# The order of the step lists of a two-layer graph kernel, head, loop and tail written anew

## The chip, the core and the metric

The kernel runs on one core of one Trainium2 chip. It is one launch that handles all 32 batches. The metric is device time in microseconds; the time before is the median of three runs.

The core's engines run side by side, each through its own list of instructions in order: TensorE (PE, matmuls), VectorE (DVE), ScalarE (ACT), GpSimd (POOL) and the queue of SyncE (SP), which issues most transfers. An engine that waits for another's result holds up everything behind in its own list, and nothing else.

## The reference

The inputs are x (32 batches of 512 x 1024) and one matrix adj (512 x 512) that serves as weight in both layers; all in float32. Cut to what matters:

```
# layer 0: attention over the 1024 columns, with rank-one scores
q = einsum('c,bcn->bn', wq, x);  k = einsum('c,bcn->bn', wk, x)
scores = leaky_relu(q[:, None, :] + k[:, :, None], 0.01)
agg = einsum('bcn,bmn->bcm', x, softmax(scores, -1))
x = layernorm(x + relu(einsum('oc,bcm->bom', adj, agg) + bm[:, None]))
# layer 1
x = layernorm(x + einsum('bnf,nm->bmf', x, adj * adj) + bias)
```

## The kernel before, in words

The attention matrix is never formed. As a score is q plus k, and the slope changes where the sum changes sign, the softmax of a column is a sum over all columns with a larger q, with one weight, and over the rest with another. So the kernel sorts the columns by q, builds running sums of the weighted columns from both ends, and looks up for each k the two running sums at its place. Per batch b, with the names of the steps as the lists have them (the dictionary `ops` gives the function of each, and a word such as `z.0.2` is step `z`, batch 0, part 2):

- `ld` (L87) loads x in four transfers. x has four buffers, so four batches are in flight. `pa` (L247) forms q and k on PE, `pc` copies them out, `co` turns them, `cc` (L267) copies the columns. `qw` (L275) writes q as a row to DRAM, and `ro` (L283) reads it back for all 128 partitions into qb, which has one buffer.
- `rk` (L308, DVE, eight parts) finds each column's rank by q, `re` makes them whole numbers; `ct` (L323, ACT, eight parts) counts for each k the columns on its other side, `ce` ends it.
- `z` (L346, PE) is the product of x and adj for 128 columns, and `zc` (L352, ACT) copies it into the table zt, of which there is one. In batches 1 to 30 only parts 0 to 3 are formed so; the other half is formed by a scheme of seven quarter products (`zU`, `zV`, `zY`, `z11`, `zZ`, `z12`, `z21`, L390) with sums `x1` to `x4` on DVE before, and copies or additions (`zUc`, `zVc`, `zZc`, `zup`, `zlr`, `zll`) between and after.
- `sc` (L451, POOL, eight parts) scatters the rows of zt to their ranks in DRAM. `tb` (L289) reads the largest q back, `tp` forms the differences to it, `we` their weights. `sl` (L470) loads the sorted rows, in two halves, into the one tile tab. `se` gives their weights.
- `u` (L491) and `d` (L501), eight each, are the running sums up and down within a partition; the first of each is ACT's. `cu` and `cd` (L509, PE) carry them over the partitions; `uc`, `te`, `dc` copy the carries; `tu` and `td` (L538, DVE) add them. `tw` (L553) and `tl` (L556) write the table to DRAM.
- `g` (L563, POOL, eight parts) gathers two rows for each column. `mw` forms the mixing weights; `ms` (L585, ACT) and `mx` (L590, DVE) mix. `t` (L609, PE) turns the result, `r` (L617, DVE) adds x, `s0` (L600, ACT), `rt`, `rce` and `n0` (L635, ACT) are the first layernorm, in four parts.
- Layer 1 is again seven products per half (`U`, `V`, `Y`, `11`, `Z`, `12`, `21`, L665, L667 and L702), twice, with `t1` to `t4` (L646 to L660) before them and copies and sums (`Uc`, `Vc`, `Zc`, `up`, `lr`, `ll`, `ls`) behind. `s1`, `ra`, `rb`, `r1` and `n` are the second layernorm, the small ones on POOL, and `st` (L777) stores the batch in four parts.

Nothing is moved by a scheduler. The order of the words in three lists of text, `head`, `loop` and `tail`, is the order in which the steps are written out, and each engine's own order is the words of its steps in that order. Buffers follow from it too: PSUM has four slots for z, q and k, the carries and the layer 1 sums, and two double ones for the quarter pairs, the turned results and the layer 1 pairs, and a tile takes a slot whose last user stands earlier in the lists. `emit` (L802) writes a list out with a base added to the batch numbers: the head with 0, the loop for each b of a range, the tail with 32. In the kernel before, the head has 2439 words, the loop 194, written five times, and the tail 2787. Where two scatters follow each other on POOL, a tiny memset (L449) is put between.

Of the kernel before, what the change touches and what calls it, by code (L numbers as in the profile page):

```python
# [49 lines left out]
def adj_resnorm_kernel(  # L50
# [759 lines left out]
    ld.0 ldw.0 pa.0 pc.0 qw.0 ld.1 wt.0 ro.0 ld.3 wd.0 wc.0 co.0 z.0.2 cc.0 rk.0.0 ct.0.2 pa.1  # L810
    zc.0.2 x3.1 ct.0.3 rk.0.7 z.0.3 ct.0.1 rk.0.4 ct.0.6 rk.0.1 ct.0.7 oq.0 rk.0.5 z.0.5 ct.0.5
    rk.0.6 R.0 z.0.4 zc.0.5 ct.0.0 pc.1 rk.0.2 qw.1 ld.2 rk.0.3 co.1 z.0.0 re.0 cc.1 bias.0
    sc.0.5 z.0.7 zc.0.0 zc.0.3 ct.0.4 sc.0.3 ro.1 sc.0.0 z.0.1 zc.0.7 zc.0.4 sc.0.4 rk.1.1
    ct.1.3 sc.0.2 z.0.6 zc.0.1 x1.1 ct.1.6 rk.1.0 sc.0.7 x2.1 rk.1.6 z11.1 sc.0.1 zc.0.6 rk.1.5
    zU.1 sc.0.6 rk.1.7 pa.2 rk.1.2 x4.1 zZ.1 rk.1.3 pc.2 zUc.1 qw.2 ct.1.4 tb.0 sl.0.0 zV.1
    sl.0.1 ct.1.1 ct.1.0 z.1.2 x1.2 ce.0 rk.1.4 zVc.1 tp.0 se.0.0 zZc.1 z.1.3 u.0.0 u.0.1 u.0.2
    se.0.1 ct.1.7 u.0.3 x2.2 co.2 ct.1.5 zY.1 u.0.4 oq.1 u.0.5 zc.1.3 ct.1.2 cc.2 z12.1 u.0.6
# [466 lines left out]
```

## Time and profile before

| | |
|---|---|
| median of three runs | 1941.6 us (1938.44 to 1947.02) |
| the profiled execution | 1942.71 us |
| its span in the trace | 1940.9 us, 23403 instructions |
| mean granted TensorE clock | 0.993 |
| busy: PE, DVE, ACT, POOL | 1887.8, 1704.6, 1483.5, 897.2 us |
| HBM read and written | 287.08 and 269.42 MB, 287 GB/s over the span |

The profile is one execution. Its busy times are sums over the span, so they hide where an engine waits: the kernel has a start in which batches come in one after the other, a long middle in which four batches overlap, and an end in which they run out. Views of a stretch (busy time by window, the timeline of one engine, the chain of waits) answer for the stretch. A bracket at the end of a timeline row gives the idle time before it and what ended it.

### The profile page before, as it was taken

To read this page: it belongs to the slowest core of one execution; us is meant where nothing else is said; L and a number is where in the kernel's file an instruction comes from. 1 tells how busy PE (TensorE), PEld (TensorE's weight loads), DVE (VectorE), ACT (ScalarE), POOL (GpSimd) and SP (SyncE) were. 2 spreads that over 40 slices of the span, in tenths; PEclk is the share of its full clock that TensorE was granted. 3 is DMA by queue.
4 is the path that set the end of the run, shared out by engine and by line. 5 is a ranking of instruction groups with operands and counts; after the bars stand their busy time and mean duration, and the time that the engine had idled before them with its cause. 6 is when DMAs were issued, how large, how long until landed. Compare 5 with 4: busy or idle time off the path is not lost.

```text
span 1940.9 us, 23403 instructions
## 1 busy us (share of the span) xinstructions
PE 1887.8 (97%) x7073; PEld 1072.0 (55%) x7073; DVE 1704.6 (88%) x2746; ACT 1483.5 (76%) x2663; POOL 897.2 (46%) x1074
## 2 busy tenths in 40 slices
PE   7988999999999999999999999999999999999897
PEld 3654555555555555566555566555565555554443
DVE  6897899998899889989988989988998989889973
ACT  3566677878778777778787778787777787877786
POOL 5263435335434345454456454455443355445531
PEclk9999999999999999999999999999999999999899
DMA  6577788677888687877787887777888677887862
GB/s 250 197 290 271 286 309 339 253 294 282 313 310 315 252 309 270 331 307 291 290 306 280 317 311 304 277 299 286 308 312 310 262 291 300 308 320 279 331 245 95
DMA packets 147446, 558.05 MB, mean 288 GB/s; under 512 B 19653, under 2 KB 19793, under 8 KB 139129
## 3 DMA queue, kind: packets, MB, share of 16 engines
q1 hardware_dynamic: 89936, 354.40, 48.4%
q0 software_dynamic: 57344, 202.15, 27.6%
q8 instruction: 56, 0.92, 0.2%
q14 instruction: 70, 0.57, 0.1%
q10 hardware_dynamic: 40, 0.02, 0.0%
HBM read 287.08 MB, written 269.42 MB: 287 GB/s over the span
## 4 chain that ended last, share of the span: by engine, by line
PE 78%; DMA 8%; DVE 7%; issue 2%; ACT 2%; POOL 2%; SPq 0%; POOLq 0%; DVEq 0%; ACTq 0%
PE z_ps L346 19%; PE sum_ps L667 18%; PE pair_ps L667 10%; PE z_sum_ps L390 9%; PE z_pair_ps L390 7%; PE pair_ps L702 5%; PE agg_ps L609 4%; DMA table<-tab 3%; PE qk_ps L247 3%; DMA tab<-sorted_z 2%; DVE tab L538 2%; PE carry_ps_True L509 1%; PE carry_ps_False L509 1%; DMA x<-in_x_dram 1%; DMA sorted_z<-zt,to 1%
## 5 line engine op out<-in xcount | busy, mean ns | idle before, releaser
L563 POOL DMA_INDIRECT got<-table,of x256 | 302.3, 1181 | 568.8 <-DMA table<-tab 260.6
L346 PE MATMUL z_ps<-adj_t,x 128*128 128x512 f32 x1088 | 486.9, 594 | 1.4 <-DVE qkc L267 1.1
L451 POOL DMA_INDIRECT sorted_z<-zt,to x256 | 314.0, 1226 | 176.7 <-issue 73.9
L308 DVE SCALAR_TENSOR_TENSOR junk_v<-qb,qkc,tie 128x1024 uint8<-128x1024 f32 x256 | 329.8, 1288 | 10.0 <-DMA qb<-q_row 6.4
L346 PEld LDWEIGHTS z_ps<-adj_t,x 128*128 128x128 f32 x1088 | 202.3, 190 | 225.5 <-issue 212.4
L323 ACT ACTIVATE junk_s<-qb,qkc 128x1024 uint8<-128x1024 f32 x256 | 293.4, 1146 | 19.7 <-DMA qb<-q_row 14.3
L667 PE MATMUL sum_ps<-zt,S 128*128 128x512 f32 x512 | 236.1, 593 | 3.1 <-DVE zt L651 1.4
L585 ACT ACTIVATE got<-got,w 128x512 f32<-128x512 f32 x256 | 172.6, 718 | 42.2 <-DVE w L580 41.8
L590 DVE SCALAR_TENSOR_TENSOR got<-got,w 128x512 f32<-128x512 f32 x256 | 185.6, 746 | 12.0 <-ACT got L585 11.8
L491 DVE SCALAR_TENSOR_TENSOR tab<-tab,ac 128x514 f32<-128x514 f32 x192 | 144.6, 753 | 49.8 <-ACT tab L486 29.2
L617 DVE SCALAR_TENSOR_TENSOR x<-agg_ps,small,x 128x1024 f32<-128x1024 f32 x128 | 163.1, 1280 | 23.9 <-PE agg_ps L609 23.6
L600 ACT ACTIVATE junk<-g,tv 128x1024 uint8<-128x1024 f32 x128 | 146.9, 1148 | 32.9 <-DVE g L722 26.4
L501 DVE SCALAR_TENSOR_TENSOR tab<-tab,ac 128x513 f32<-128x513 f32 x224 | 167.5, 748 | 2.6 <-ACT tab L499 1.9
L667 PEld LDWEIGHTS sum_ps<-zt,S 128*128 128x128 f32 x512 | 96.5, 190 | 121.6 <-issue 105.8
L753 POOL TENSOR_SCALAR tv<-tv 128x1 f32<-128x1 f32 x124 | 53.1, 428 | 238.5 <-ACT junk L600 230.5
L774 ACT ACTIVATE g<-g,nb,tv 128x1024 f32<-128x1024 f32 x124 | 151.0, 1237 | 7.3 <-POOL nb L764 7.2
L600 ACT ACTIVATE junk<-x,tv 128x1024 uint8<-128x1024 f32 x128 | 146.9, 1148 | 12.2 <-DVE x L617 9.9
L538 DVE TENSOR_TENSOR tab<-tab,carry 128x2052 f32<-128x2052 f32 x64 | 146.2, 2291 | 4.7 <-ACT carry L516 4.7
L635 ACT ACTIVATE x<-x,tv 128x1024 f32<-128x1024 f32 x128 | 139.3, 1141 | 0.5
L609 PEld LDWEIGHTS agg_ps<-ident,got 128*128 128x128 f32 x1024 | 116.4, 141 | 36.2 <-issue 24.9
L609 PE MATMUL agg_ps<-ident,got 128*128 128x128 f32 x1024 | 129.4, 274 | 2.7 <-DVE g L722 2.0
L667 PE MATMUL sum_ps<-x,adj 128*128 128x512 f32 x256 | 123.3, 605 | 7.4 <-ACT x L635 7.4
(144 smaller groups left out, 3281.5 us busy)
## 6 DMA issues: line engine op xcount, KB each, us to landing
table<-tab SPq DMA_DIRECT2D x64, 2056.0 KB
tab<-sorted_z SPq DMA_DIRECT2D x64, 1028.0 KB
x<-in_x_dram SPq DMA_DIRECT2D x128, 512.0 KB
out_dram<-g SPq DMA_DIRECT2D x128, 512.0 KB
qb<-q_row SPq DMA_DIRECT2D x32, 512.0 KB
sorted_z<-zt,to POOLq DMA_INDIRECT x256, 5.0
got<-table,of POOLq DMA_INDIRECT x256, 8.0
adj_in<-in_adj_dram SPq DMA_DIRECT2D x1, 1024.0 KB
```

Source lines behind the costliest of these rows:

```text
L308: nc.vector.scalar_tensor_tensor(s.junk, s.qb, s.q[:, j : j + 1], tie[:, at : at + N], ALU.subtract, ALU.is_gt, accum_out=s.rank[:, j : j ...
L323: nc.scalar.activation(junk, s.qb, AF.Sign, bias=s.k[:, j : j + 1], accum_out=s.sign[:, j : j + 1])
L346: nc.tensor.matmul(s.z[j], xt[:, c, j * P : (j + 1) * P], adj_t[:, c, :], start=(c == 0), stop=(c == CT - 1),)
L390: nc.tensor.matmul(ps, a[:, i, k * P : (k + 1) * P], v[:, i, :], start=start and i == 0 and (k == 0 or bank == 1), stop=(i == 1), skip_gro ...
L451: nc.gpsimd.indirect_dma_start(out=sorted_z[b % 2][:, :], out_offset=bass.IndirectOffsetOnAxis(ap=s.to[:, j : j + 1], axis=0), in_=zt[:, j ...
L538: nc.vector.tensor_tensor(v, v, c, ALU.add)
L563: nc.gpsimd.indirect_dma_start(out=s.got[:, j, :], out_offset=None, in_=table[b % 2][:, :], in_offset=bass.IndirectOffsetOnAxis(ap=s.of[:, ...
L585: nc.scalar.activation(down, down, AF.Copy, scale=s.w[:, 1, j : j + 1])
L590: nc.vector.scalar_tensor_tensor(up, up, s.w[:, 0, j : j + 1], down, ALU.mult, ALU.add)
L600: nc.scalar.activation(junk, t, AF.Square, bias=v[0][:, i : i + 1], scale=-float(N), accum_out=v[1][:, i : i + 1],)
L609: nc.tensor.transpose(s.agg[o][:, j * P : (j + 1) * P], s.got[:, j, o * P : (o + 1) * P], ident)
L667: nc.tensor.matmul(ps, a[:, k, g * P : (g + 1) * P], v[:, k, :], start=False, stop=(k == 1), skip_group_check=first is None,)
```

## The change

The three lists are replaced by others. Both programs hold the same 6196 steps, each on its engine; the place of the steps in the order differs. The head now has 2633 words and the loop is written eight times, for batches 15 to 22 in place of 14 to 18; the tail has 2011. As fewer scatters stand next to each other, 161 of the small memsets are there in place of 164. Shown are the start of the head, its part around the first layer 1, the whole loop, and a part of the tail; the rest is of the same kind.

```diff
     head = """
-    ld.0 ldw.0 pa.0 pc.0 qw.0 ld.1 wt.0 ro.0 ld.3 wd.0 wc.0 co.0 z.0.2 cc.0 rk.0.0 ct.0.2 pa.1
-    zc.0.2 x3.1 ct.0.3 rk.0.7 z.0.3 ct.0.1 rk.0.4 ct.0.6 rk.0.1 ct.0.7 oq.0 rk.0.5 z.0.5 ct.0.5
-    rk.0.6 R.0 z.0.4 zc.0.5 ct.0.0 pc.1 rk.0.2 qw.1 ld.2 rk.0.3 co.1 z.0.0 re.0 cc.1 bias.0
-    sc.0.5 z.0.7 zc.0.0 zc.0.3 ct.0.4 sc.0.3 ro.1 sc.0.0 z.0.1 zc.0.7 zc.0.4 sc.0.4 rk.1.1
-    ct.1.3 sc.0.2 z.0.6 zc.0.1 x1.1 ct.1.6 rk.1.0 sc.0.7 x2.1 rk.1.6 z11.1 sc.0.1 zc.0.6 rk.1.5
-    zU.1 sc.0.6 rk.1.7 pa.2 rk.1.2 x4.1 zZ.1 rk.1.3 pc.2 zUc.1 qw.2 ct.1.4 tb.0 sl.0.0 zV.1
-    sl.0.1 ct.1.1 ct.1.0 z.1.2 x1.2 ce.0 rk.1.4 zVc.1 tp.0 se.0.0 zZc.1 z.1.3 u.0.0 u.0.1 u.0.2
-    se.0.1 ct.1.7 u.0.3 x2.2 co.2 ct.1.5 zY.1 u.0.4 oq.1 u.0.5 zc.1.3 ct.1.2 cc.2 z12.1 u.0.6
-    zlr.1 zc.1.2 ro.2 u.0.7 z.2.2 re.1 zup.1 d.0.7 d.0.6 sc.1.4 x3.2 d.0.5 sc.1.2 cu.0 d.0.4
-    z21.1 d.0.3 te.0 sc.1.3 uc.0 tl.0 ct.2.2 tu.0.0 z.1.0 we.0 zll.1 d.0.2 ct.2.4 sc.1.7 rk.2.1
...
-    tu.1.0 zc.3.3 cd.1 zVc.3 dc.1 zY.3 oq.3 ct.3.7 mx.0.7 sc.3.1 td.1.0 ct.3.5 z12.3 ms.0.6
-    td.1.1 z.3.0 ms.0.5 tw.1.0 ms.0.4 tu.1.1 zc.3.0 zlr.3 tw.1.1 mx.0.5 tb.2 z21.3 mx.0.6 mx.0.4
-    zup.3 zll.3 t.0.2 r.0.2 t.0.1 sc.3.4 r.0.1 sc.3.7 t.0.3 s0.0.2 r.0.3 sc.3.0 t.0.0 s0.0.1
-    r.0.0 sc.3.6 s0.0.3 sl.2.0 sl.2.1 tp.2 sc.3.5 s0.0.0 g.1.3 rt.0 rce.0 n0.0.0 g.1.2 n0.0.1
-    g.1.1 se.2.0 U.0.0 t1.0 g.1.0 u.2.0 n0.0.2 u.2.1 u.2.2 n0.0.3 g.1.5 u.2.3 U.0.1 t2.0 Uc.0.0
-    g.1.7 se.2.1 t4.0 11.0.0 Uc.0.1 g.1.4 u.2.4 t3.0 V.0.0 g.1.6 u.2.5 mw.1.0 Z.0.0 sc.3.2
-    Vc.0.0 u.2.6 ms.1.0 u.2.7 ms.1.1 sc.3.3 Y.0.0 ce.3 mx.1.0 Zc.0.0 d.2.7 mx.1.1 ms.1.3 d.2.6
-    11.0.1 d.2.5 mw.1.1 12.0.0 d.2.4 ms.1.5 tb.3 lr.0.0 ms.1.2 mx.1.3 V.0.1 mx.1.2 d.2.3 Z.0.1
-    Vc.0.1 up.0.0 ms.1.7 mx.1.5 21.0.0 tp.3 Zc.0.1 d.2.2 ms.1.6 ms.1.4 12.0.1 ll.0.0 mx.1.4
...
+    ld.0 ldw.0 ld.1 bias.0 pa.0 pc.0 qw.0 wt.0 wd.0 wc.0 co.0 z.0.2 ro.0 x1.1 cc.0 pa.1 rk.0.2
+    ct.0.0 rk.0.7 z.0.4 pc.1 ct.0.4 qw.1 rk.0.5 zc.0.2 ct.0.5 rk.0.0 ct.0.1 co.1 rk.0.1 z.0.0
+    ct.0.3 cc.1 rk.0.3 ct.0.6 rk.0.6 ct.0.7 z.0.5 rk.0.4 zc.0.4 ct.0.2 re.0 x2.1 oq.0 ro.1
+    sc.0.4 ld.2 z.0.3 zc.0.5 sc.0.5 sc.0.2 rk.1.3 ct.1.3 z.0.1 zc.0.3 R.0 ct.1.7 zc.0.0 sc.0.0
+    z.0.7 zc.0.1 ce.0 x3.1 sc.0.3 rk.1.0 sc.0.1 rk.1.6 z.0.6 zc.0.7 rk.1.2 ct.1.1 sc.0.7 rk.1.5
+    ct.1.6 x4.1 pa.2 zc.0.6 sc.0.6 z11.1 pc.2 ct.1.5 qw.2 zU.1 tb.0 sl.0.0 sl.0.1 co.2 zUc.1
+    zZ.1 tp.0 ct.1.4 rk.1.7 zV.1 zZc.1 rk.1.1 ct.1.2 z.1.2 x1.2 zVc.1 se.0.0 rk.1.4 u.0.0 ct.1.0
+    u.0.1 u.0.2 se.0.1 ro.2 z.1.3 zc.1.2 u.0.3 ld.3 x2.2 u.0.4 oq.1 cc.2 u.0.5 u.0.6 z12.1
+    zc.1.3 re.1 u.0.7 d.0.7 zY.1 zup.1 d.0.6 sc.1.4 cu.0 zlr.1 z.2.2 d.0.5 uc.0 sc.1.3 x3.2 te.0
+    d.0.4 tl.0 sc.1.5 d.0.3 x4.2 d.0.2 z21.1 rk.2.1 z.1.0 zll.1 d.0.1 ct.2.0 sc.1.7 d.0.0 ce.1
...
+    ct.3.4 r.0.2 t.0.1 sc.3.5 r.0.1 sc.3.0 t.0.3 s0.0.2 r.0.3 sc.3.7 t.0.0 s0.0.1 r.0.0 sc.3.4
+    s0.0.3 sl.2.0 sl.2.1 tp.2 sc.3.6 s0.0.0 g.1.3 rt.0 rce.0 n0.0.1 g.1.2 n0.0.0 g.1.1 se.2.0
+    U.0.1 g.1.0 u.2.0 n0.0.3 u.2.1 g.1.4 t1.0 n0.0.2 u.2.2 g.1.5 U.0.0 t2.0 u.2.3 g.1.7 11.0.0
+    Uc.0.0 t4.0 Uc.0.1 se.2.1 t3.0 g.1.6 V.0.0 u.2.4 ce.3 mw.1.0 11.0.1 sc.3.2 u.2.5 ms.1.1
+    ms.1.0 u.2.6 Z.0.0 ms.1.3 u.2.7 Vc.0.0 mx.1.3 d.2.7 mx.1.1 V.0.1 Zc.0.0 d.2.6 d.2.5 Y.0.0
+    mw.1.1 d.2.4 ms.1.6 12.0.0 ms.1.2 lr.0.0 ms.1.7 mx.1.0 ms.1.5 mx.1.2 Z.0.1 ms.1.4 up.0.0
+    d.2.3 21.0.0 Zc.0.1 mx.1.5 zc.3.3 d.2.2 mx.1.6 12.0.1 ll.0.0 mx.1.4 Vc.0.1 s1.0.0 ls.0.0
+    d.2.1 Y.0.1 ld.4 mx.1.7 s1.0.2 ra.0.0 cu.2 lr.0.1 ra.0.2 rb.0.0 up.0.1 t.1.2 uc.2 r1.0.0
+    sc.3.3 21.0.1 te.2 r.1.2 s1.0.1 d.2.0 t.1.1 n.0.0 ra.0.1 rb.0.2 t.1.3 r.1.1 ll.0.1 rb.0.1
+    cd.2 s0.1.2 r1.0.2 r1.0.1 tu.2.0 t.1.0 tb.3 s0.1.1 tl.2 z.4.3 st.0.0 r.1.3 dc.2 n.0.2 ls.0.1
+    tp.3 td.2.0 s1.0.3 st.0.2 zU.4 s0.1.3 ra.0.3 r.1.0 tw.2.0 rb.0.3 pa.4 r1.0.3 td.2.1 s0.1.0
+    we.3 z.4.2 tu.2.1 pc.4 n.0.3 qw.4 rt.1 st.0.3 rce.1 x1.4 n0.1.3 tw.2.1 z11.4 ro.4 zc.4.2
...
     """
     loop = """
-    z.0.0 s0.-3.0 x2.0 x3.0 rt.-3 tp.-1 rce.-3 ct.0.6 rk.0.7 ct.0.5 zV.0 oq.0 rk.0.2 g.-2.3
-    sl.-1.0 sl.-1.1 rk.0.3 zZ.0 zVc.0 g.-2.0 x4.0 zY.0 rk.0.6 zZc.0 g.-2.1 n0.-3.0 rk.0.0
-    n0.-3.1 z12.0 g.-2.2 zlr.0 n0.-3.2 t1.-3 U.-3.0 g.-2.5 n0.-3.3 re.0 zup.0 se.-1.0 ct.0.1
-    z21.0 sc.0.4 u.-1.0 sc.0.5 11.-3.1 Uc.-3.0 u.-1.1 ct.0.4 t2.-3 g.-2.7 zll.0 11.-3.0 u.-1.2
-    se.-1.1 u.-1.3 g.-2.6 V.-3.0 u.-1.4 mw.-2.0 g.-2.4 u.-1.5 ms.-2.2 U.-3.1 Vc.-3.0 u.-1.6
-    sc.0.6 ce.0 t3.-3 Z.-3.0 Uc.-3.1 sc.0.7 u.-1.7 ms.-2.3 ms.-2.0 sc.0.2 ms.-2.1 Z.-3.1 d.-1.7
-    mx.-2.1 sc.0.3 we.-1 mx.-2.2 Zc.-3.0 V.-3.1 d.-1.6 Zc.-3.1 mx.-2.3 d.-1.5 12.-3.1 Vc.-3.1
-    mw.-2.1 t4.-3 ms.-2.4 12.-3.0 ms.-2.6 up.-3.1 ms.-2.7 Y.-3.0 d.-1.4 ld.1 s1.-3.1 mx.-2.6
-    zc.0.1 ra.-3.1 Y.-3.1 zc.0.0 lr.-3.0 rb.-3.1 ms.-2.5 up.-3.0 r1.-3.1 sc.0.1 21.-3.0 lr.-3.1
-    s1.-3.0 sc.0.0 mx.-2.5 d.-1.3 21.-3.1 ll.-3.0 ra.-3.0 mx.-2.7 n.-3.1 rb.-3.0 d.-1.2 cu.-1
-    r1.-3.0 mx.-2.4 ll.-3.1 st.-3.1 d.-1.1 pa.1 uc.-1 ls.-3.1 ls.-3.0 d.-1.0 s1.-3.3 tu.-1.0
-    z.1.2 s1.-3.2 ra.-3.3 mx.-2.0 pc.1 rb.-3.3 te.-1 tu.-1.1 qw.1 tl.-1 r1.-3.3 t.-2.2 ro.1
-    zc.1.2 n.-3.0 cd.-1 ra.-3.2 r.-2.2 rb.-3.2 co.1 n.-3.3 t.-2.1 r1.-3.2 st.-3.0 cc.1 t.-2.3
-    dc.-1 r.-2.1 st.-3.3 n.-3.2 tb.0 z.1.3 td.-1.0 s0.-2.1 st.-3.2 ct.1.3 r.-2.3 tw.-1.0 ct.1.2
-    z.1.1 td.-1.1 zc.1.3 ct.1.7 rk.1.5 s0.-2.3 tw.-1.1 t.-2.0 x1.1 ct.1.0 zU.1 rk.1.4 r.-2.0
-    z11.1 zUc.1 s0.-2.2 rk.1.1
+    z.0.0 x3.0 zUc.0 x2.0 rt.-3 ct.0.5 oq.0 rk.0.7 rce.-3 rk.0.3 zV.0 g.-2.0 sl.-1.0 sl.-1.1
+    x4.0 zZ.0 rk.0.0 zVc.0 g.-2.3 ct.0.6 rk.0.2 zY.0 zZc.0 n0.-3.1 g.-2.1 tp.-1 rk.0.6 n0.-3.0
+    z12.0 g.-2.2 zlr.0 n0.-3.3 t1.-3 U.-3.0 g.-2.5 se.-1.0 n0.-3.2 re.0 zup.0 ct.0.1 z21.0
+    sc.0.4 u.-1.0 sc.0.5 11.-3.1 Uc.-3.0 u.-1.1 ct.0.4 t2.-3 g.-2.4 se.-1.1 11.-3.0 u.-1.2 zll.0
+    u.-1.3 g.-2.7 V.-3.0 u.-1.4 mw.-2.0 g.-2.6 u.-1.5 ms.-2.2 U.-3.1 Vc.-3.0 u.-1.6 sc.0.7 t3.-3
+    Z.-3.0 Uc.-3.1 u.-1.7 sc.0.6 ms.-2.0 mx.-2.2 ms.-2.3 ms.-2.1 Z.-3.1 sc.0.3 d.-1.7 mx.-2.1
+    Zc.-3.0 d.-1.6 sc.0.2 we.-1 V.-3.1 mx.-2.3 Zc.-3.1 d.-1.5 mw.-2.1 12.-3.1 t4.-3 ms.-2.7
+    Vc.-3.1 12.-3.0 ms.-2.4 up.-3.1 ms.-2.6 d.-1.4 s1.-3.1 Y.-3.0 ld.1 mx.-2.6 zc.0.1 ra.-3.1
+    zc.0.0 rb.-3.1 Y.-3.1 lr.-3.0 ms.-2.5 r1.-3.1 up.-3.0 sc.0.1 21.-3.0 lr.-3.1 sc.0.0 s1.-3.0
+    mx.-2.5 d.-1.3 21.-3.1 ra.-3.0 ll.-3.0 mx.-2.7 n.-3.1 rb.-3.0 d.-1.2 cu.-1 r1.-3.0 mx.-2.4
+    ll.-3.1 d.-1.1 pa.1 uc.-1 ls.-3.0 ls.-3.1 d.-1.0 s1.-3.3 tu.-1.0 z.1.2 te.-1 ra.-3.3 s1.-3.2
+    tl.-1 mx.-2.0 st.-3.1 rb.-3.3 tu.-1.1 pc.1 n.-3.0 qw.1 r1.-3.3 t.-2.2 st.-3.0 zc.1.2 ro.1
+    cd.-1 ra.-3.2 r.-2.2 n.-3.3 rb.-3.2 co.1 t.-2.1 r1.-3.2 dc.-1 cc.1 ce.0 st.-3.3 n.-3.2
+    t.-2.3 tb.0 r.-2.1 z.1.3 st.-3.2 td.-1.0 ct.1.0 s0.-2.1 r.-2.3 tw.-1.0 ct.1.2 z.1.1 rk.1.5
+    ct.1.7 td.-1.1 zc.1.3 ct.1.3 t.-2.0 s0.-2.3 rk.1.4 tw.-1.1 zU.1 s0.-2.2 x1.1 r.-2.0 z11.1
+    rk.1.1 s0.-2.0
     """
     tail = """
...
-    z.-1.6 r.-4.0 g.-3.6 rk.-1.2 g.-3.1 oq.-1 r.-4.1 se.-2.0 z.-1.4 u.-2.0 g.-3.5 we.-3 u.-2.1
-    s0.-4.1 u.-2.2 g.-3.3 zc.-1.5 ce.-1 u.-2.3 se.-2.1 re.-1 s0.-4.0 g.-3.2 z.-1.7 u.-2.4 u.-2.5
-    zc.-1.4 g.-3.0 rt.-4 u.-2.6 rce.-4 ce.-2 n0.-4.3 u.-2.7 g.-3.4 d.-2.7 zc.-1.7 d.-2.6 sc.-1.0
-    zc.-1.2 cu.-2 n0.-4.1 d.-2.5 d.-2.4 g.-3.7 n0.-4.0 d.-2.3 uc.-2 U.-4.1 mw.-3.0 sc.-1.7
-    zc.-1.6 d.-2.2 te.-2 tu.-2.1 n0.-4.2 tl.-2 sc.-1.2 st.-5.3 ms.-3.2 11.-4.1 n.-5.0 d.-2.1
-    mw.-3.1 n.-5.1 U.-4.0 st.-5.0 sc.-1.1 d.-2.0 ms.-3.6 t1.-4 st.-5.1 sc.-1.6 ms.-3.1 cd.-2
...
+    rt.-4 rce.-4 zc.-1.7 d.-2.7 g.-3.5 cu.-2 n0.-4.1 d.-2.6 g.-3.6 d.-2.5 zc.-1.4 n0.-4.0 d.-2.4
+    sc.-1.4 ce.-2 uc.-2 d.-2.3 U.-4.0 n.-5.0 mw.-3.0 sc.-1.2 d.-2.2 te.-2 U.-4.1 st.-5.0 tu.-2.1
+    n0.-4.2 sc.-1.1 n0.-4.3 d.-2.1 n.-5.1 11.-4.1 mw.-3.1 sc.-1.6 ms.-3.2 d.-2.0 st.-5.1 st.-5.3
+    t1.-4 cd.-2 tl.-2 sc.-1.0 11.-4.0 tu.-2.0 dc.-2 ms.-3.1 sc.-1.7 ms.-3.6 Z.-4.1 td.-2.0
+    ms.-3.3 Uc.-4.1 sc.-1.3 Z.-4.0 Zc.-4.1 mx.-3.3 tw.-2.0 ms.-3.4 t2.-4 ms.-3.7 ms.-3.5 mx.-3.1
+    V.-4.1 ms.-3.0 td.-2.1 12.-4.1 Vc.-4.1 Zc.-4.0 mx.-3.6 Uc.-4.0 tw.-2.1 mx.-3.4 12.-4.0
...
     """
     weights()
     emit(head, 0)
-    for b in range(14, 19):
+    for b in range(15, 23):
         emit(loop, b)
     emit(tail, B)
```

## The prediction

> **What bounds the kernel now.** I read the page first: the busy line, then the slices by time.
>
> ```profile
> PE 1887.8 (97%) x7073; PEld 1072.0 (55%) x7073; DVE 1704.6 (88%) x2746; ACT 1483.5 (76%) x2663; POOL 897.2 (46%) x1074
> PE   7988999999999999999999999999999999999897
> DVE  6897899998899889989988989988998989889973
> ```
>
> TensorE is full except in the first five slices and the last three; VectorE comes second at 88%. How much is to be had is asked of the stretches, in the busy time by window (columns: PE, weight loads, DVE, ACT, POOL, then granted clock and DMA):
>
> ```profile
> 100.00:150.00 50.00, 41.72 (x148) 25.23 (x147) 44.67 (x73) 32.55 (x62) 35.56 (x35) 0.97 0.78 296
> 150.00:200.00 50.00, 46.48 (x177) 24.67 (x176) 40.18 (x65) 35.67 (x62) 13.23 (x21) 1.00 0.73 283
> 1000.00:1050.00 50.00, 50.00 (x202) 29.89 (x202) 44.87 (x71) 39.79 (x71) 24.39 (x25) 1.00 0.80 305
> 1800.00:1850.00 50.00, 43.72 (x123) 21.39 (x122) 48.30 (x72) 39.11 (x70) 27.75 (x29) 0.91 0.83 312
> 1850.00:1900.00 50.00, 45.54 (x154) 22.74 (x153) 37.21 (x61) 42.08 (x69) 17.27 (x26) 1.00 0.57 222
> ```
>
> In the middle PE has no hole: batch 17's `pa` starts at 1000.0 and batch 18's at 1058.3, 58.2 us for one batch. The undisturbed rows of a batch give the same: 2.1 for `pa` and `co`, 4 `z` of 3.43, 7 quarter products of 1.73, `cu` and `cd` 0.87 each, 4 `t` of 0.87, and twice (2 x 1.93 + 5 x 1.72) for layer 1: 58.05. Thirty of these are 1741.5; batches 0 and 31 (8 `z`, no quarters) 59.7 each; turning adj 3.0: 1863.9 in all. The first matmul starts at 6.8 and the last ends at 1929.3, so PE loses about 59 us. I placed them by comparing each step's start-to-start time with its undisturbed row: 7 in 0 to 50, 18 in 50 to 250, 12 or 13 in the 1500 us between, 22 from 1750 on. Another order can win no more than these, and some of it not: the first wait for adj (4.5) is a load. The matmul engine's timeline shows the largest waits:
>
> ```profile
> 147.28 3.39 PE L667 MATMUL sum_ps<-x,adj 128*128 128x512 f32 x4 [4.41 <-ACT x L635]
> 154.93 2.18 PE L702 MATMUL pair_ps<-x,adj 128*128 128x512 f32 x4 [2.33 <-issue]
> 1798.18 3.19 PE L667 MATMUL sum_ps<-x,adj 128*128 128x512 f32 x4 [1.65 <-ACT x L635]
> 1834.25 2.08 PE L509 MATMUL carry_ps_True<-end,before 128*128 128x257 f32 x4 [4.16 <-DVE end L491]
> ```
>
> Each is a chain of short steps on other engines with no matmul left to put between: turn, residual, spread, root, norm for `U.0`; load, sums for `cu.31`. The rows of 3.39 and 3.19 us are 1.88 elsewhere: they run at the half clock that follows an idle PE. The chain of waits adds the load behind the second one:
>
> ```profile
> 143.21 16.59 DMA tab<-sorted_z
> ```
>
> **The change, part by part.** The same 6196 steps stand in another order; three of the 164 spacer memsets (L449, 90 ns) fall away, which POOL at 46% doesn't notice. So nothing is saved in work, and the sum is only of waits removed and waits made. I laid the new lists along the trace of before with its own durations, stretch by stretch.
>
> *Start to 48 us.* `ld.1` goes ahead of `qw.0`, `ld.3` far back, `bias.0` ahead of all DVE work. The bias steps (5.45 us) leave 37.6 for the idle time before 13.8; but at 37.6 DVE was waiting for the second q row until 43.1, so they cost nothing there either. Here the Trainium skill speaks against the change.
>
> ```profile
> 10.86 0.61 SPq L275 DMA_DIRECT2D q_row<-part  x1
> 13.44 0.44 SPq L283 DMA_DIRECT2D qb<-q_row  x1
> ```
>
> By this row alone the q row is read back 2.6 us after it is written, so qb would again be issued at 13.4 and follow `ld.1`'s 2 MB, landing at about 20.3 (20.9 now). "DMA: Bandwidth & Descriptors", section "Queues, rings and completion order", says that an engine of the DMA consumes descriptors in ring order: then the q row itself waits behind `ld.1`. x_0 took from 1.9 to 7.3 us, so x_1 behind adj runs from about 12 to 17.4, the q row lands near 17.9, qb is issued at 18.3 and lands near 21.3. I take this: 0.4 later, on DVE and ACT alone; PE has `z.0` to do. PE gains `z.0.0` to `z.0.7` without the wait for `cc.1` (1.2 with its start): `z.0.6` ends at 46.8, not 48.2. What would cost more is `ld.2`, now behind `ro.1`: issued at about 33.5, landed at 41, wanted at 47. Sum: -1.3.
>
> *48 to 142.* Batch 0's sorted rows can be loaded when `sc.0.6` is through, 1.2 earlier, but `tp.0` now stands in front of four steps of DVE and waits to about 55.7; `u.0.7` ends at 67.7 (69.4), and PE, which has less in front of `cu.0`, is there at 66.4. A wait of 1.3 takes the gain. From `tw.0.1` on (89.8 against 90.0) the gathers, and with them `mx.0` and `t.0.2`, stand at 137 to 137.8 as before. Sum here: +1.3.
>
> *142 to 177.* `U.0.1` comes first, and `n0.0.1` before `n0.0.0`; the first matmul reads the rows of `n0.0.0`, one ACT norm (1.04) later. `se.2.0` and `u.2.0` still stand before `n0.0.2`, so the 2.3 before `11.0.0` stays. But `11.0.1` and `V.0.1` now fill the time before `Y.0.0`, and `t3.0` no longer waits behind `u.2.4`. `cu.2` ends at about 176.3 (177.1). Sum: -0.8.
>
> *177 to 231.* The one large move. `zc.3.3` goes behind eight `ms.1` (172 instead of 125), and `sc.3.3` behind `ra.0.0` to `r1.0.0` on POOL, where it ran at 158.6:
>
> ```profile
> 166.75 0.33 SPq L289 DMA_DIRECT2D top<-sorted_z  x1
> 177.84 0.19 POOL L753 TENSOR_SCALAR tv<-tv 128x1 f32<-128x1 f32 x1 [18.24 <-ACT junk L600]
> ```
>
> So `tb.3`, issued at 166.75 now, can't go before some 184, and behind it on SP stand `tl.2`, the stores of batch 0, `tw.2.0`, `qw.4`, `ro.4`; behind `tp.3` on DVE stand `td.2.0`, `r.1.0`, `td.2.1`, `tu.2.1`. DVE reaches `tp.3` at 184.7 and waits to about 187.2; `tw.2.1` goes at 195.5 (193.4), `sl.3` lands 2.1 later, `se.3.0` holds ACT to 211.6, and `zZc.4` behind it holds `z12.4` for 1.6. The old 0.9 before `zY.4` goes. After `12.1.1` I am at 231.2 against 230.4: +0.8 from the start. The bounds: nothing if the scatter lands in 5 us; +4 if it takes 10, as from `sc.1.1` (82.9) to `tb.1` (93.3). I take +0.8.
>
> *231 to 1750.* Here I shifted the slack of each PE step behind its producer by the row time that the new order puts in front of either. Waits that go: 0.97 at 299, 0.73 at 417, 0.9 at 687, 2.6 together. Waits that come: `z21.24` 1.0, `U.24.0` 1.4, `zY.30` 1.5, `co.31` 1.1, together 5.0. This overstates, as a producer is late in part because PE is; I take half of the difference, +1.2 (bounds -3 and +5). The loop itself (8 turns for 5) keeps all its margins.
>
> *1750 to the end.* `n0.28.3` moves behind `n0.28.0`, and PE starts `U.28` 0.8 earlier. It is given back: DVE is dense from 1795 to 1834 in the same steps, and `cu.31` waits for `u.31.7` at 1834 whichever way PE got there. From `U.30` on both lists keep PE full, and the 11.6 from last matmul to last store are the same. Sum: 0.
>
> In all +2.0 on the profiled execution of 1942.71 (span 1940.9): 1944.7. The median of the three runs, 1941.6, lies 1.1 below that execution, so 1943.6 in its terms; the half that I discounted at `co.31` is behind the wait for `cu.31` too (1.1), which gives 1942.5.
>
> **The rivals.** *Faster.* The filling at 142 to 177 works at each starved place: a third of the 40 us lost in 50 to 250 and after 1750 is 13, 1929. For it: in each stretch a second half's matmul stands ready. Against it: the longest waits are chains on DVE and DMA that keep their length, and the walk finds fillers at one place.
>
> *Slower, by the norms.* `n0.b.1` stands before `n0.b.0` in 22 batches instead of 7, 17 of them new, and `U.b.0` reads `n0.b.0` first. In the loop its margin falls from 1.62 to 0.58 us. Up to 0.58 of lateness on ACT this costs nothing; past it PE loses all of it in each of 17 batches, unless it is made up: at 1.2 us late (0.6 lost a batch) 10 us, 1953. It decides from there. Against it: PE is full in the middle and ACT at 39.8 of 50 can catch up.
>
> *Slower, by `tb.3`.* If it lands near 197 instead of 187 nothing covers it: one for one, +10, 1952. For it: two queues stand behind it. Against it: SP's old row there is idle from 176.5 to 184.8.
>
> *The q row isn't held up.* Then DVE starts 1 us earlier and PE doesn't notice: 1942, no case of its own.
>
> **How the numbers follow.** No change 0.62, faster 0.16, slower by norms 0.13, by `tb.3` and other new waits in lists walked only by slack 0.09. 0.5% is 9.7 us, about what measurement can tell: below 1931.9 and above 1951.3. So faster 0.16, same 0.62, slower 0.22. I predict 1942.5. The range takes in most of both sides, 1930 to 1956, and leaves about 0.09 out at each end.
>
> **What would show it.** Right: `z.0.6` ends near 47, `cu.0` waits a little; `tb.3` goes at 184 or later and `tp.3` waits; `U.0` again waits over 4 us; 58.2 per batch in the loop; the 4 us before `cu.31` stay. Wrong: a batch in the loop over 58.5, PE busy under 1880 with waits for L635, or those waits at 150 and 1834 gone.

## The result, and the profile after

The changed kernel takes 1950.33 us (median of 12 runs, 1946.32 to 1956.42) against 1941.83 for the kernel before in 12 runs: a ratio of 1.0041, with a 95% interval of 1.003 to 1.0053. It is 8.5 us slower. The time lies within the range given (1930 to 1956) and in the class given the most chance, within 0.5%; the predicted 1942.5 is 7.8 us too low. The interval does not contain 1, so the slowdown is real.

The profiled execution took 1946.32 us, the fastest of its twelve, against 1942.71 for that of the kernel before. So the trace holds 3.6 us of the 8.5. The page, busy line and slices of PE and DVE:

```profile
span 1944.6 us, 23407 instructions
PE 1888.9 (97%) x7073; PEld 1073.5 (55%) x7073; DVE 1707.7 (88%) x2746; ACT 1477.9 (76%) x2663; POOL 903.4 (46%) x1071
PE   7998999999999999999999999999999999999797
DVE  6897898998889998999988999988999989999973
```

The work is the same: PE differs by 1.1 us, DVE by 3. Only POOL, at 46% of the span, is busy for 6 us more (903.4 against 897.2). By window of the changed kernel (columns: PE, weight loads, DVE, ACT, POOL, granted clock, DMA share, GB/s):

```profile
0.00:50.00 50.00, 37.08 (x142) 18.13 (x143) 33.63 (x63) 18.18 (x32) 27.83 (x31) 0.93 0.53 184
100.00:150.00 50.00, 44.07 (x161) 27.35 (x159) 46.48 (x76) 30.53 (x60) 32.86 (x35) 0.99 0.78 292
150.00:200.00 50.00, 46.50 (x172) 24.98 (x173) 38.66 (x62) 33.63 (x62) 18.54 (x22) 0.94 0.69 267
1000.00:1050.00 50.00, 50.00 (x204) 30.07 (x203) 45.52 (x74) 39.70 (x73) 25.38 (x27) 1.00 0.84 317
1800.00:1850.00 50.00, 39.55 (x113) 18.74 (x112) 47.27 (x75) 36.80 (x68) 23.77 (x32) 0.93 0.81 314
1850.00:1900.00 50.00, 45.45 (x149) 22.40 (x148) 38.47 (x61) 41.59 (x67) 17.03 (x28) 1.00 0.60 233
```

and the same first window of the kernel before:

```profile
0.00:50.00 50.00, 39.45 (x158) 19.48 (x159) 33.22 (x66) 19.47 (x33) 27.39 (x37) 0.97 0.69 247
```

The middle is as full as it was. The first window has lost 2.4 us of PE's time and stands at a clock of 0.93; 16 matmuls fewer are done by 50 us. Counted as in the prediction, start to start against the undisturbed rows, PE loses 12.0 us up to the end of `z.0.6` instead of 6.8. The timeline of VectorE says why:

```profile
11.60 0.41 DVE L213 CAST bias_part<-bias_in 6x512 bf16<-6x512 f32 x1 [4.49 <-DMA table<-zero]
13.16 1.14 DVE L213 CAST bias_part<-bias_in 6x512 bf16<-6x512 f32 x1
15.10 1.51 DVE L219 SCALAR_TENSOR_TENSOR bias_in<-bias_part,small,bias_in 6x512 f32<-6x512 bf16 x1
18.68 0.56 DVE L222 CAST bias_p<-bias_in 6x512 bf16<-6x512 f32 x1
19.17 1.27 DVE L183 COPY adj_t<-adj_tp 128x512 f32<-128x512 f32 x2
```

`bias.0` (L205 to L222), now the first work of VectorE after the setup, starts its small steps at 6.5 and then waits from 7.1 to 11.6 for a transfer that has nothing to do with the bias: the store of a row of zeros. `bias_part` and that row are tiles of one tag, "end", which has one buffer. Then it takes 7.6 us, to 19.2, for what took 5.0 in the kernel before (38.1 to 43.1). Behind it stands `wd.0` (L183), the copy of two parts of the turned adj, which could have gone at about 13. And PE waits for that. The row of the changed kernel, then that of the kernel before:

```profile
20.59 6.49 PE L346 MATMUL z_ps<-adj_t,x 128*128 128x512 f32 x8 [4.09 <-DVE adj_t L183]
```

```profile
16.98 3.72 PE L346 MATMUL z_ps<-adj_t,x 128*128 128x512 f32 x8 [0.25 <-ACT adj_t L179]
```

`z.0.2` comes 3.6 us later and, after the wait, its eight matmuls take 6.49 us instead of 3.72: the granted clock between 20.6 and 27.0 us is 0.56. `z.0.6`, the last product of batch 0, ends at 53.4 (48.3).

At the other places that the prediction showed, the waits of `U.0` and of `cu.31` are there as before, and the wait for the late `tb.3` came as forecast. The row at 1843.85, `11.29.0`, is taken up further down.

```profile
151.59 3.75 PE L667 MATMUL sum_ps<-x,adj 128*128 128x512 f32 x4 [5.45 <-ACT x L635]
1836.54 2.08 PE L509 MATMUL carry_ps_True<-end,before 128*128 128x257 f32 x4 [4.96 <-DVE end L491]
1843.85 1.98 PE L702 MATMUL pair_ps<-x,adj 128*128 128x512 f32 x4 [1.81 <-ACT x L635]
187.08 0.33 SPq L289 DMA_DIRECT2D top<-sorted_z  x1
189.58 0.15 DVE L296 TENSOR_SCALAR top<-top 128x1 f32<-128x1 f32 x1 [1.83 <-DMA top<-sorted_z]
```

### The profile page after: what moved, and what is told of

The parts are those of the page before. It is cut to its first block, busy times and chain, and to the rows that moved or that the text cites. A ratio compares the mean times of both kernels' runs of the same rounds, so it can differ in the third digit from the quotient of the medians.

```text
span 1944.6 us, 23407 instructions
## 1 busy us (share of the span) xinstructions
PE 1888.9 (97%) x7073; PEld 1073.5 (55%) x7073; DVE 1707.7 (88%) x2746; ACT 1477.9 (76%) x2663; POOL 903.4 (46%) x1071
## 4 chain that ended last, share of the span: by engine, by line
PE 81%; DMA 8%; DVE 6%; issue 2%; ACT 2%; POOL 1%; DVEq 0%; ACTq 0%; SPq 0%; POOLq 0%
PE z_ps L346 21%; PE sum_ps L667 19%; PE pair_ps L667 10%; PE z_sum_ps L390 9%; PE z_pair_ps L390 7%; PE agg_ps L609 5%; PE pair_ps L702 5%; PE qk_ps L247 3%; DMA table<-tab 2%; DMA tab<-sorted_z 2%; DVE tab L538 2%; DMA got<-table,of 2%; PE carry_ps_True L509 1%; PE carry_ps_False L509 1%; POOL got L563 1%
## 5 line engine op out<-in xcount | busy, mean ns | idle before, releaser
L451 POOL DMA_INDIRECT sorted_z<-zt,to x256 | 309.0, 1207 | 171.8 <-issue 67.3
L590 DVE SCALAR_TENSOR_TENSOR got<-got,w 128x512 f32<-128x512 f32 x256 | 186.2, 747 | 10.5 <-ACT got L585 10.0
L600 ACT ACTIVATE junk<-g,tv 128x1024 uint8<-128x1024 f32 x128 | 146.8, 1147 | 40.2 <-DVE g L722 34.4
L600 ACT ACTIVATE junk<-x,tv 128x1024 uint8<-128x1024 f32 x128 | 146.9, 1148 | 19.2 <-DVE x L617 12.2
```

The source lines that it names most:

```text
L451: nc.gpsimd.indirect_dma_start(out=sorted_z[b % 2][:, :], out_offset=bass.IndirectOffsetOnAxis(ap=s.to[:, j : j + 1], axis=0), in_=zt[:, j ...
L590: nc.vector.scalar_tensor_tensor(up, up, s.w[:, 0, j : j + 1], down, ALU.mult, ALU.add)
L600: nc.scalar.activation(junk, t, AF.Square, bias=v[0][:, i : i + 1], scale=-float(N), accum_out=v[1][:, i : i + 1],)
```

## The experiments

Each kernel was timed in five rounds against the kernel before on the same chip. The first four shared their runs of it (1942.51), the next four (1943.53), the last four (1942.39). Ratios carry their 95% interval; 0.001 is 1.94 us. Runs of different groups are compared by their ratios. Words of the lists that a diff does not need are left out.

### Where the loss is: the changed kernel again, and bias.0 moved in both orders

The changed kernel again, without an edit:

> The changed kernel once more, for a second profile: the first profiled execution (1946.3) lies 4.0 us under the median of its twelve runs (1950.3), so half of the slowdown is in no profile yet. If the loss is that of the start alone (z.0.6 ends 5.1 us later, 2.6 of it left at 250 us), the difference to the kernel before up to 250 us is again 2 to 3 us and the rest comes at random places. If the new order of the loop and the tail is itself slower, this profile shows more than 60.5 us between pa.24 and pa.25 or over 58.5 us per batch in the loop.

Measured: 1949.19, ratio 1.0037 [1.0023, 1.0051]. Its profiled execution took 1946.28, once more the fastest. `bias.0` waits in it for the same store to 10.5, `wd.0` goes at 19.0, `z.0.6` ends at 51.8. A batch of the loop takes 58.2 as before, and neither of the two profiles has new waits in the loop (batches 15 to 22).

`bias.0` late in the new order, against the changed kernel:

```diff
-    ld.0 ldw.0 ld.1 bias.0 pa.0 pc.0 qw.0
+    ld.0 ldw.0 ld.1 pa.0 pc.0 qw.0
...
-    oq.0 ro.1 sc.0.4
+    oq.0 bias.0 ro.1 sc.0.4
```

> bias.0 behind oq.0 instead of at the very start; nothing else. Theory 'start' (bias.0 holds wd.0 on VectorE, z.0.2 waits 4.1 us and runs 3.0 us at the half clock): wd.0 runs at about 13.8, z.0.6 ends near 48, some 5 us earlier, and 2.6 us of that reaches the end: about 1947.7. Rival 'chain' (the chain up to U.0 at 155 has other causes and takes the gain): z.0.6 near 48, t.0.2 still at 141, and 1950.

Measured: 1942.28, ratio 0.9995 [0.9989, 1.0002]. The whole slowdown is gone, with one word of 6196. Both theories had expected a slower kernel than this: the one word is worth about 8 us of the median. `wd.0` goes at 13.0, and PE follows without a wait:

```profile
14.98 3.70 PE L346 MATMUL z_ps<-adj_t,x 128*128 128x512 f32 x8 [0.46 <-ACT adj_t L179]
```

`z.0.6` ends at 45.0 (53.4 in the changed kernel, 48.3 in the one before); `t.0.2` starts at 134.4 (141.1 with `bias.0` early).

The old order with `bias.0` first, against the kernel before:

```diff
-    ld.0 ldw.0 pa.0 pc.0 qw.0 ld.1 wt.0
+    ld.0 ldw.0 bias.0 pa.0 pc.0 qw.0 ld.1 wt.0
...
-    re.0 cc.1 bias.0
+    re.0 cc.1
```

> The kernel before with bias.0 moved to the start alone. Theory 'start': the store of zeros stands behind adj there, bias.0 ends near 19, z.0.2 starts near 20.6 instead of 17.0 and at the half clock, +5 us at 48 us and +2 to +3 at the end: about 1944.5. If it is ld.1 ahead of the stores of zeros that makes them late, bias.0 ends before 15 here and the time stays at 1942.

Measured: 1945.43, ratio 1.0017 [1.0009, 1.0024]. The same move costs 3.3 us there. `bias.0` waits for the zeros to 10.5 here too, though `ld.1` is not ahead of them, so it is not `ld.1` that makes the store late.

### What makes bias.0 late: the buffer

The order of the changed kernel is kept; the zeros lie in an unused part of the buffer of the bias rows.

```diff
-    room = one.tile([P, NT, 2 * ZR], F32, tag="tab", name="bias_in")[0:6, :, 0:H]
+    room_all = one.tile([P, NT, 2 * ZR], F32, tag="tab", name="bias_in")
+    room = room_all[0:6, :, 0:H]
...
-    zero = one.tile([P, ZR], F32, tag="end", name="zero")[0:1, :]
+    zero = room_all[0:1, 2, 0:ZR]
```

> bias.0 stays first, but the row of zeros for the two tables lies in an unused part of the buffer of the bias rows instead of in the buffer that bias.0 writes its parts to. If bias.0 is late because of that buffer (its wait of 4.5 us to 11.6, when the second store of zeros has landed), it ends at 13 to 15 instead of 19.2, z.0.2 starts near 17, and the time is that of e2 (1947.7). If it waits for the bias rows themselves, it starts again at 11.6 and the time is 1950.

Measured: 1943.22, ratio 0.9997 [0.9987, 1.0007], the same as with `bias.0` late as far as the intervals tell. The timeline of VectorE in that run (lines are one higher):

```profile
7.12 0.42 DVE L214 CAST bias_part<-bias_in 6x512 bf16<-6x512 f32 x1
9.74 0.73 DVE L220 SCALAR_TENSOR_TENSOR bias_in<-bias_part,small,bias_in 6x512 f32<-6x512 bf16 x1
11.72 0.41 DVE L223 CAST bias_p<-bias_in 6x512 bf16<-6x512 f32 x1
13.17 0.69 DVE L184 COPY adj_t<-adj_tp 128x512 f32<-128x512 f32 x1 [1.03 <-PE adj_tp L175]
```

`bias.0` starts at 7.1 and ends at 12.1, in 5.0 us, before adj is turned. The bias rows had landed by 7.1. So the idea behind the place, to use VectorE while it waits for adj, was sound; the shared buffer undid it.

`bias.0` behind `wd.0`, against the changed kernel:

```diff
-    ld.0 ldw.0 ld.1 bias.0 pa.0 pc.0 qw.0 wt.0 wd.0 wc.0
+    ld.0 ldw.0 ld.1 pa.0 pc.0 qw.0 wt.0 wd.0 bias.0 wc.0
```

> The changed kernel with bias.0 one step later on VectorE, behind wd.0 instead of in front of it: bias.0 is still early and still slow beside POOL's work. If it is wd.0, and through it z.0 and the last scatter of batch 0, that carries the loss, z.0.6 ends near 45 to 46 and the time is that of bias.0 late, 1942 to 1943. If an early bias.0 costs by holding up VectorE's ranks (they would start at 21 to 22 instead of 20.3), 1945 or more.

Measured: 1948.49, ratio 1.0035 [1.0022, 1.0048]. The first of the two expectations fell. `wd.0` goes at 12.3 and `z.0.2` at 14.2, but now the rest is behind `bias.0`:

```profile
15.03 1.41 DVE L215 TENSOR_TENSOR bias_in<-bias_in,bias_part 6x512 f32<-6x512 f32 x1
19.01 1.75 DVE L219 SCALAR_TENSOR_TENSOR bias_in<-bias_part,small,bias_in 6x512 f32<-6x512 bf16 x1
23.87 1.37 DVE L222 CAST bias_p<-bias_in 6x512 bf16<-6x512 f32 x1
25.95 1.15 ACT L323 ACTIVATE junk_s<-qb,qkc 128x1024 uint8<-128x1024 f32 x1 [11.79 <-DVE qkc L267]
27.51 0.44 PE L262 MATMUL qk_tp<-ident,part 128*128 128x128 f32 x2 [4.09 <-ACT part L255]
```

`bias.0` takes 11.4 us (13.8 to 25.2), and `cc.0` behind it comes at 25.8. `ct.0.0` on ACT waits for that, `pc.1` behind `ct.0.0`, `co.1` on PE for `pc.1`, and `z.0.0` stands behind `co.1`. `z.0.6` ends at 50.2. The path is another one, the loss nearly the same: what costs is a slow `bias.0` in front of the work of batch 0, be it `wd.0` or `cc.0`. The two places that cost nothing in these runs are before adj lands (with its own zeros) and behind the ranks of batch 0.

Set side by side, with the times read from the traces:

| kernel | bias.0 | z.0.6 ends | t.0.2 starts | median us | ratio to before |
|---|---|---|---|---|---|
| before | 37.6 to 43.1 | 48.3 | 137.8 | 1941.8 | 1 |
| old order, bias.0 first | 6.4 to 18.2 | 51.2 | 140.4 | 1945.4 | 1.0017 |
| changed | 6.5 to 19.2 | 53.4 | 141.1 | 1950.3 | 1.0041 |
| changed, again | 6.5 to 19.1 | 51.8 | 139.7 | 1949.2 | 1.0037 |
| changed, behind wd.0 | 13.8 to 25.2 | 50.2 | 139.0 | 1948.5 | 1.0035 |
| changed, own zeros | 6.6 to 12.1 | 46.4 | 135.6 | 1943.2 | 0.9997 |
| changed, bias.0 late | 34.6 to 40.2 | 45.0 | 134.4 | 1942.3 | 0.9995 |

Each time but the median is of one execution, and these vary. Six of the kernels in this text have `bias.0` late, with the same order up to `t.0.2` but for the moves of `tb.3`; in their traces `z.0.6` ends at 44.3 to 47.9 and `t.0.2` starts at 134.4 to 136.3. Against the trace with `bias.0` late, the three slow kernels of the new order are 5.2 to 8.4 us behind at `z.0.6` and 4.6 to 6.6 at `t.0.2`, and 6 to 8 us by their medians; in the old order it is 2.9, 2.6 and 3.3.

What hands the delay on is PE itself. Between the end of `z.0.6` and `t.0.2` it has 85.1 us of matmuls in every kernel, by the undisturbed rows. The changed kernel takes 87.7 us for this stretch, the kernel before 89.6, the one with `bias.0` late 89.5. So a late start leaves out about 2 us of waiting and nothing more. Then PE has to wait for the residual, the spread and the norm of batch 0, and that wait doesn't shrink for a late PE, as they start from `t.0`: the first matmul of layer 1 that reads x comes 10.5 us after `t.0.2` in both. With `bias.0` late its row shows a wait of 5.66, where the changed kernel has 5.45 (the row at 151.59 above).

```profile
144.95 3.75 PE L667 MATMUL sum_ps<-x,adj 128*128 128x512 f32 x4 [5.66 <-ACT x L635]
```

### Is the rest of the change slower: parts of the two orders joined

The lists agree closely on what is done by `pa.5` (240 us) and by `pa.31` (1760 us), so they can be joined there. The new head with `bias.0` late, then the old order (the diff is against the changed kernel, and leaves out the move of `bias.0`):

```diff
     n.1.0 t.2.1 ls.1.1 tu.3.0 pa.5
-    s1.1.3 d.3.3 s1.1.2 ra.1.3 r.2.2 z.5.2 pc.5
+    s1.1.3 ra.1.3 d.3.3 r.2.1 z.5.2 pc.5 s1.1.2
...
```

> The new head with bias.0 behind oq.0, up to pa.5 (240 us), then the old order to the end. In the profile of the run with bias.0 late, pa.6 starts 5.9 us earlier than in the kernel before, but its time is the same: either the new order of the rest loses what the head wins, and this run keeps it, at 1937 (5 faster than before); or the old rest absorbs it too (the load before cu.31, the chains at 1460 and 1800), and it is 1941 to 1942.

Measured: 1940.95, ratio 0.9987 [0.9976, 0.9998]: 2.5 us faster than before, between the two expectations.

The old order up to `pa.5`, then the new one, against the changed kernel:

```diff
...
-    n.1.0 t.2.1 ls.1.1 tu.3.0 pa.5
+    t.2.1 ls.1.1 tu.3.0 s1.1.3 pa.5
     te.3 rb.1.1 ce.4 n.1.0 d.3.3 s1.1.2
```

> The old order up to pa.5, then the new one of loop and tail. If the new rest costs 5 us, as the first case above says, 1947; if it costs nothing, 1942 to 1943. The forecast of the prediction for this part was +1.2.

Measured: 1942.68, ratio 0.9995 [0.9984, 1.0005]. From 240 us on the new order costs nothing that this can tell, +1 us at most.

The new order with `bias.0` late up to `pa.31`, then the old tail, against the kernel with `bias.0` late:

```diff
     r1.27.0 ls.27.1 d.29.1 ra.27.1 pa.31
-    uc.29 d.29.0 ra.27.2 s1.27.3 ce.29 r.28.2
+    ce.29 s1.27.3 ra.27.3 d.29.0 rb.27.3 r.28.2
...
```

> The new order with bias.0 late up to pa.31 (1760 us), then the old order of the last 170 us. The profile shows 2 us more of waits for the new order between 1750 and the end: if these are real the time is 1940; if the loss of the rest lies in the loop or is nowhere, 1942.

Measured: 1941.04, ratio 0.9992 [0.9983, 1.0], which doesn't differ from the run with the new tail (0.9995). In the traces the new tail is slower by a little: from the end of `cu.31` to the end of the last matmul it is 91.8 to 93.1 in the six traces with the old tail and 93.4 to 94.5 in the eight with the new. It lies between `21.28.1` and `11.29.0`, where the changed kernel's PE loses 3.7 us instead of 1.7 because the norm for `11.29.0` is late (the row at 1843.85 above).

### The other terms: tb.3, the norms, ld.1

`tb.3` early, against the kernel with `bias.0` late:

```diff
-    te.1 tu.1.0 ct.3.5
+    te.1 tu.1.0 zc.3.3 ct.3.5
...
-    ms.1.1 ms.1.0 u.2.6
+    ms.1.1 ms.1.0 sc.3.3 u.2.6
...
-    mx.1.0 ms.1.5 mx.1.2
+    mx.1.0 ms.1.5 tb.3 mx.1.2
...
-    d.2.3 21.0.0 Zc.0.1 mx.1.5 zc.3.3 d.2.2
+    d.2.3 21.0.0 tp.3 Zc.0.1 mx.1.5 d.2.2
...
-    uc.2 r1.0.0 sc.3.3 21.0.1
+    uc.2 r1.0.0 21.0.1
...
-    tu.2.0 t.1.0 tb.3 s0.1.1
+    tu.2.0 t.1.0 s0.1.1
...
-    n.0.2 ls.0.1 tp.3 td.2.0
+    n.0.2 ls.0.1 td.2.0
```

> The new order with bias.0 late, and zc.3.3, sc.3.3, tb.3 and tp.3 put back to where the old one has them. The prediction charged the move with about 1.6 (z12.4 waiting for ACT) to 2.1: then 1940.5. If SP's queue and VectorE have the room, as the profile suggests (12.1.1 ends 53.0 us behind cu.2 in the new and 53.4 in the old order), 1942.

Measured: 1941.59, ratio 0.999 [0.9981, 0.9999] against 0.9995 with `tb.3` late. The difference, 1 us, has the sign of the forecast of 1.6 to 2.1 and about half its size, but the intervals overlap, so it isn't settled.

The norms of 17 batches, in the new order with `bias.0` late; batch 20 stands for all:

```diff
-    zY.23 zZc.23 n0.20.1 g.21.1 tp.22 rk.23.6 n0.20.0 z12.23
+    zY.23 zZc.23 n0.20.0 g.21.1 tp.22 rk.23.6 n0.20.1 z12.23
...
```

> The new order with bias.0 late; in the 17 batches where the old order has n0.b.0 before n0.b.1 and the new one after it, the two change places again. If the rival 'norms' holds (PE waits for n0.b.0 in many batches), the time falls by up to 10, to 1932, and the 1410 us between pa.6 and pa.30 by as much; if the loop's margin of 0.58 us is enough, as the profile of the new kernel suggests (58.2 per batch), it stays at 1941 to 1942.

Measured: 1943.09, ratio 1.0005 [0.9997, 1.0013], against 0.9995 without this edit. Nothing is won by the old order of the norms: the 10 us of this rival are not there.

`ld.1` ahead in the old order, against the kernel before:

```diff
-    ld.0 ldw.0 pa.0 pc.0 qw.0 ld.1 wt.0
+    ld.0 ldw.0 ld.1 pa.0 pc.0 qw.0 wt.0
```

> The kernel before with ld.1 ahead of qw.0 alone. If the q row waits behind the 2 MB of ld.1, qb is issued at about 17 instead of 13.4; lands about as before, and the ranks start at 20 to 21 as before, so no change: 1942.5. If qb lands 3.7 us later too, DVE's ranks and with them the scatters of batch 0 are 3 to 4 us late, and that reaches the end one for one as bias.0's delay does: 1946.

Measured: 1943.47, ratio 1.0006 [0.9997, 1.0014]: no change. `qb` is issued at 17.65 instead of 13.44, the first rank starts at 22.1 instead of 21.1, and `z.0.6` ends at 48.2 (48.3).

### A kernel that beats both

The edits of three runs above in one kernel: `bias.0` late, `tb.3` early (one of its moves is shown), and the old order from `pa.5` on.

```diff
-    oq.0 ro.1 sc.0.4
+    oq.0 bias.0 ro.1 sc.0.4
...
-    mx.1.0 ms.1.5 mx.1.2
+    mx.1.0 ms.1.5 tb.3 mx.1.2
...
     n.1.0 t.2.1 ls.1.1 tu.3.0 pa.5
-    s1.1.3 d.3.3 s1.1.2 ra.1.3 r.2.2 z.5.2 pc.5
+    s1.1.3 ra.1.3 d.3.3 r.2.1 z.5.2 pc.5 s1.1.2
...
```

> New head with bias.0 late and tb.3 early, up to pa.5, then the old order: the two that came out lowest, together. If the gains add, 1939.5 (4 faster than before); if both are within what the wait before cu.31 varies by (4.3 to 6.7), 1941.

Measured: 1937.84 (1933.39 to 1940.68), ratio 0.9978 [0.9969, 0.9987]: 4.3 us faster than the kernel before and some 12 faster than the changed one. The gains add, as near as this can tell. It joins the parts that had come out lowest, so some of its gain may be chance.

## Why the prediction was right or wrong

The class and the range held, but in part by luck: the range reached to 1956 for the norms and `tb.3`, and neither made the slowdown. The forecast of no visible change failed, by one step above all.

*Start to 48 us: -1.3 forecast, +5.1 in the first trace and +3.5 in the second.* The failed sentence is that the bias steps "leave 37.6 for the idle time before 13.8" and "cost nothing there either". Three things were not looked at: that `bias_part` waits for the buffer of the zeros, to 11.6; that what is then left of the idle time is some 1.5 us for 5 us of work; and that `wd.0` and `cc.0` stand behind it on VectorE, with PE behind them (4.1 us for `wd.0` in the changed kernel, 4.3 for `cc.0` in the old order with `bias.0` first). The 5.45 us themselves were right for VectorE alone. The shared buffer could be read in the text of the kernel (the two tiles' tag); how late the store lands would have had to be bounded. Without this term the start is as forecast: `z.0.6` at 44.3 to 47.9 in the six traces with `bias.0` late, where I had 46.8.

*The q row.* The row of the kernel before gave 13.4 for `qb`; my estimate by the order that the Trainium skill states ("DMA: Bandwidth & Descriptors", section "Queues, rings and completion order") was 18.3. It was 17.2, and 17.65 with `ld.1` moved alone: the traces agree with the page, and that PE doesn't notice was right too (1.0006). `ld.2` was issued at 39.3, 5.8 later than I put it, and PE lost nothing by it.

*48 to 142: +1.3 forecast, -1.8 measured* (+5.1 at `z.0.6`, +3.3 at `t.0.2`). This step is wrong in the mechanism too. I let a wait of 1.3 at `cu.0` take the gain of the start, and put `t.0.2` at 137 to 137.8 as before. In the changed kernel PE comes late and doesn't wait there. With `bias.0` late the wait at `cu.0` is 0 to 0.6 in five traces and 1.5 in one, and `t.0.2` starts at 134.4 to 136.3: most of the gain gets through.

*142 to 177: -0.8 forecast, -0.6 measured* (+2.7 at the end of `cu.2`), with the wait of over 4 us before `U.0` that was named.

*177 to 231: +1.6 forecast (from -0.8 to +0.8), -0.3 measured* (+2.5). The steps came as told: `tb.3` at 187.1 (184 or later), `tp.3` waits 1.8, `tw.2.1` at 197.9 (195.5), and `se.3.0` ends at 213.2 (211.6), with all of it some 2 us late from the start. The wait before `z12.4` is 0.5 instead of 1.6, and the 0.9 before `zY.4` is gone as forecast. The run with `tb.3` early leaves 0 to 2 us for it.

*231 to 1750: +1.2 forecast, -0.2 measured.* The old waits at 299, 417, 670 and 687 are gone. Of the four new ones that I named, only that at `co.31` came (0.6); others did (1.5 at `Y.3.1`, 1.0 at `V.5.0`), of another size in each trace. The loop takes 58.2 a batch. Joined to the old head this part measures as the old one.

*The tail: 0 forecast, +1.5 in the trace.* The gain of `U.28` was given back at `cu.31`, as told. The 2 us before `11.29.0` were not seen.

With the first step's +5.1 in place of its -1.3 the sum would be 1942.5 + 6.4 = 1948.9, against 1950.3. That this comes so near is in part luck. The five other terms were +3.3 together in the prediction, and in the trace they are about -1.3: there the last matmul ends 3.7 later than in the kernel before, not 8.4. Apart from the second, wrong by 3.1, each of them is off by 2 us or less. The last step of the sum also takes off 1.1 for `co.31`, of which the halved difference had counted only half.

*The rivals.* The norms fell by their own experiment, and `tb.3` went at 187 and had landed at 189.6, not near 197. Faster did not happen, but the filling that speaks for it is real: with `bias.0` out of the way the joined kernel is at 0.9978. The slowdown came by a way that no rival named. Of the signs named for being right, `z.0.6` near 47 and a wait at `cu.0` failed and the others came; none of the signs of being wrong appeared.

*What stays open.* Both profiles of the changed kernel are of executions 3 to 4 us under their medians, while that of the kernel before is at its median. So no trace shows a typical execution of the changed kernel. The trace with `bias.0` late is 2.5 under its own median; between it and the changed kernel's, 6.5 of the 8 us are seen, about what `t.0.2` shows. Some waits vary between traces of like orders: that for adj at 12 from 3.1 to 4.9, that before `cu.31` from 4.3 to 6.7. Whether these make the 3 to 4 us was not settled. Nor was it tried what makes the store of zeros take to 11.6. The store is two transfers. The chain of waits of the changed kernel puts the second behind the load of the bias rows, and both of these small transfers take nearly 5 us:

```profile
2.05 4.68 DMA bias_in<-in_L_gnn_bias_dram
6.75 4.77 DMA table<-zero
```

In the old order with `bias.0` first that second one is issued at 6.0 already and still holds `bias.0` to 10.5.

## What to carry to other kernels

Before a step is moved into an idle stretch, look at its buffers as well as its inputs: a tile of a tag with one buffer waits for that tag's last reader, here a store of 2 KB. Then look at what stands behind it on the same engine, since a step that starts late in a gap delays all of that. A delay at the start is not made good by a long full middle: here 5 to 8 us at 50 us were 6 to 8 at 1950. PE was full from then on, and the next wait, for the first layer norm of batch 0, began only once PE had come to it.

## What was not expected of the hardware

The same small steps of VectorE on 6 partitions take very different times by what POOL does beside them. L219 takes 0.73 us with `bias.0` late, 1.41 to 1.51 in the changed kernel, and 1.63 to 1.75 behind `wd.0`; all of `bias.0` from L213 on takes 5.0, 7.6 and 10.7 us. In the second trace of the changed kernel L219 takes only 0.83 and 0.93, but L215 up to 1.41 and L217 1.35 (0.68 and 0.47 in the run with its own zeros), 8.5 us in all. With `bias.0` late POOL is not idle either: it issues scatters from 35.6 to 39.5, and these slow nothing. In the slow cases, from 12.7 us on in the changed kernel, it forms the sums of adj (L186 to L193), and its own steps grow as well: the second L186 of the changed kernel takes 1.48, in the run with its own zeros (where it is L187) 1.04:

```profile
14.59 1.48 POOL L186 TENSOR_TENSOR adj<-adj_in 128x512 f32<-128x512 f32 x1
```

```profile
13.99 1.04 POOL L187 TENSOR_TENSOR adj<-adj_in 128x512 f32<-128x512 f32 x1
```

The Trainium skill, "SBUF — State Buffer", section "Who interferes with whom", has the two engines share a pair of ports as an exclusive lock, and rows that grow on both sides agree with that. These runs show only the overlap in time: POOL's work was not taken away to test it, so that the ports are the cause is not shown here.
